# Softmax denominators summed on four quarters of TensorE's columns, inverted on 128 columns, and broadcast through DRAM

## The chip, the cores and the metric

The kernel runs on one core of a Trainium2 chip. The metric is the device time of one execution in microseconds (us). A core has five engines that work side by side, each through its own instructions in order: TensorE (PE in the profile; its weight loads are the row PEld), VectorE (DVE), ScalarE (ACT), GpSimd (POOL) and SyncE (SP), which here only issues DMAs. An instruction that has to wait holds up everything behind it on its own engine.

## The reference

Two attention layers follow each other on `x` of shape (8, 512, 64, 64), in float32. The first is a softmax attention with pooled keys and values:

```python
f = conv1x1(x, Wf, bf).reshape(b, c // K, h * w)       # 64 x 4096 for each image
g = maxpool2x2(conv1x1(x, Wg, bg))                     # 64 x 1024
v = maxpool2x2(conv1x1(x, Wh, bh))                     # 256 x 1024
s = jnp.einsum('bcn,bcm->bnm', f, g)
beta = jax.nn.softmax(s, axis=-1)
o = jnp.einsum('bcm,bnm->bcn', v, beta)
x1 = gamma * conv1x1(o, Wv, bv) + x
```

The second is a linear attention on the result x1: its features are `10 * relu(q) + exp(10 * min(q, 0))`, and `x1 + gamma * (KV applied to the features, over their norm)` is the output. The change concerns the softmax of the first layer alone: for each position n, the exponentials of 1024 scores are summed, the sum is inverted, and all 1024 are multiplied by the inverse.

## The kernel before, in words

**Chunks and steps.** Each image's 4096 positions are cut into 8 chunks of 512 (`CH`), so there are 64 chunks (`TOTAL`) in 8 images. A loop over `step(s)` runs from s = -9 to 64. A step does several stages for different chunks: `project` and `attend` of chunk s; `weigh_two`, `sum_of_e`, `total`, `invert` and `normalize_block` of the next chunk n = s + 1; the first convolutions (`a_fg`, `a_h`) of chunk s + 9; and, with j = s % 8 the step's place in its image, in steps with odd j from the second image on, `finish`, which adds the second layer's result for two chunks of the image before to the output in DRAM. The last image's eight steps have no first convolutions, since no chunk is left for them, and its own second layer is finished after the loop. Here "odd step" means a step with odd j that has a `finish`.

**What sets the order.** The order is written by hand. Every piece of work is entered by `at(t, fn, ...)`, with t a time within the step, and the step emits all of it in order of t, under a manual schedule. So the order on each engine and in each queue is the order of the t's, and the numbers t matter only as an order. The dependencies (semaphores) are put in by the framework.

**The softmax of chunk n.** `weigh` makes scores on PE, two blocks at a time, and ACT takes their exponentials into `E`, an SBUF tile of 128 partitions x 8 blocks x 512 positions: the 1024 keys lie over partitions and blocks, the positions along the columns. `sum_of_e` (L432 to L437, DVE) adds the eight blocks into `r`, 128 x 512. `total` (L441) sums `r` over the partitions by a matmul with a 128 x 128 matrix of ones, so that each of 128 partitions of a PSUM bank `tot` receives the same 512 sums. `invert` (L446) takes the reciprocal of that bank into another PSUM bank, `rtot`. `look` (L450, L451, ACT) reads both banks once more for a later check that all sums and inverses are of a sane size, and `normalize_block` (L460, DVE) multiplies the four quarters of `E` by `rtot`.

**Around it in the same step.** On PE, L441 stands among the products of `attend` (L484); after those come the convolution `fg` (L259), the products N of `project` (L547) mixed with H (L303), and then `features` (`pk`, L593). On DVE, the reciprocal is followed by nine small operations of `attend` (L502 to L517), the first quarter of L460, the pooling of `fg` (L236, L267), two quarters of L460, a sum into `xb` (L563), the last quarter, three more L563 and two L568. `features` reads `xb` after L568. On ACT, `look` is followed by the evictions of `project` (L557) with the bias added, each of which POOL adds to `xb` (L560); three later products of `project` accumulate on the bank that an eviction has read. In the last image's steps `features_exp` (L603, L604) stands between `look` and the first eviction.

**The queues.** SP issues the loads of x (L212, L224), the stores (L574) and the DMA transposes of halves: of v (`turn_v`, L358), of x (L648) and of k (L630). `turn_v` is SP's next work after the point where the change puts its DMAs. The two accumulating DMAs of `finish` (L801, 1 MB each, `out_dram<-y`) are issued by POOL. In the profile's DMA lines q1 is the queue of SP's DMAs and q0 that of POOL's.

**Buffers.** PSUM is a pool of 8 banks (`bank`), and `scratch` is a pool of 7 SBUF tiles of 128 x 512.

Of the kernel before, what the change touches and what calls it, by code (L numbers as in the profile page):

```python
# [36 lines left out]
F32 = mybir.dt.float32  # L37
U16 = mybir.dt.uint16
AF = mybir.ActivationFunctionType
ALU = mybir.AluOpType  # L40
AX = mybir.AxisListType

PARAM = 10.0
EPS = 1e-10
P = 128
CH = 512
SAFE = 1e27

# [2 lines left out]
def tile_two_attention_blocks(  # L51
# [21 lines left out]
    nc = tc.nc  # L73
# [3 lines left out]
    CV = WhT.shape[1]  # L77
    KT = C // P
    VT = CV // P
    NCHUNK = N // CH  # L80
    M = N // 4
    MT = M // P
    NT = CH // P
    TOTAL = B * NCHUNK
    HN = CH // 2
    xr = x.rearrange("b (k p) h w -> b p k (h w)", p=P)
    outr = out.rearrange("b (k p) h w -> b p k (h w)", p=P)
    wv1r = wvT.rearrange("(k p) o -> p k o", p=P)

    const = ctx.enter_context(tc.tile_pool(name="const", bufs=1))  # L90
# [23 lines left out]
    for e in range(2):  # L114
        nc.scalar.dma_start(out=b_kq[e * D : (e + 1) * D, e : e + 1], in_=bk.rearrange("(p o) -> p o", o=1))
        nc.scalar.dma_start(
            out=b_kq[(1 - e) * D : (2 - e) * D, e : e + 1], in_=bq.rearrange("(p o) -> p o", o=1)
# [6 lines left out]
    ident = const.tile([P, P], F32, name="ident")  # L124
# [4 lines left out]
    ones = const.tile([P, P], F32, name="ones")  # L129
    nc.gpsimd.memset(ones, 1.0)  # L130

    kk = const.tile([P, CH], F32, name="kk")

# [29 lines left out]
    chk = const.tile([P, 2, TOTAL], F32, name="chk")  # L163
# [4 lines left out]
    def run(ctx, general):  # L168
# [6 lines left out]
        work1 = ctx.enter_context(tc.tile_pool(name="work1", bufs=1))  # L175
        work = ctx.enter_context(tc.tile_pool(name="work", bufs=2))
        temp = ctx.enter_context(tc.tile_pool(name="temp", bufs=7))
        turned = ctx.enter_context(tc.tile_pool(name="turned", bufs=1))
        small = ctx.enter_context(tc.tile_pool(name="small", bufs=4))
        psum = ctx.enter_context(tc.tile_pool(name="psum", bufs=8, space=bass.MemoryType.PSUM))  # L180

        def bank(name):
            return psum.tile([P, CH], F32, tag="m", name=name)

        def scratch(name):
            return temp.tile([P, CH], F32, tag="t", name=name)

# [38 lines left out]
        st = {}  # L226
        fgs, fs, vps = {}, {}, {}

        th, hs, es, sums, totals, rtots, te, os_, to, ns = ({} for _ in range(10))
        pxs, x_last, stored, late = [], {}, {}, {}  # L230
        kTs, xTs, pks, qq, halves, turned_halves = ({} for _ in range(6))

# [204 lines left out]
                nc.vector.tensor_tensor(r[:, 0, :], r[:, 0, :], r[:, 1, :], ALU.add)  # L437

        def total(s):
            pt = totals[s] = bank(f"tot_{s}")  # L440
            nc.tensor.matmul(pt, ones, sums[s][:, 0, :], start=True, stop=True)  # L441

        def invert(s):

            rtots[s] = bank(f"rtot_{s}")
            nc.vector.reciprocal(rtots[s], totals[s])  # L446

        def look(s):
            pt = totals[s]
            nc.scalar.activation(pt, pt, AF.Copy, accum_out=chk[:, 0, s : s + 1])  # L450
            nc.scalar.activation(pt, rtots[s], AF.Copy, accum_out=chk[:, 1, s : s + 1])  # L451

        def block(s, i, j):

# [438 lines left out]
        def step(s):  # L893
# [8 lines left out]
            def at(t, fn, *args):  # L902
                work.append((t, len(work), fn, args))
# [79 lines left out]
            if after:  # L983
                n = s + 1
                if here:
                    at(5.7, weigh_two, n, 0)
                    at(7.5, weigh_two, n, 2)
                    for m, t in ((2, 9.3), (4, 10.6), (6, 11.8), (8, 13.1)):
                        at(t, sum_of_e, n, m)

                if not here:
                    t, t_invert = 21.2, 21.25
                elif s == 0:
                    t, t_invert = 21.2, 22.6
                else:
                    t, t_invert = 16.1 if j % 2 == 1 and c_here else 17.85, 18.0
                at(t, total, n)
                at(t_invert, invert, n)
                if not general:
                    at(max(21.5, t_invert + 0.1), look, n)  # L1000
                at(24.3, normalize_block, n, 0, 1)
                at(26.0, normalize_block, n, 0, 0)
                at(27.3, normalize_block, n, 1, 1)
                at(29.2, normalize_block, n, 1, 0)
                at(33.6, sums_of_e, n, 1)
                at(36.0, sums_of_e, n, 2)
# [65 lines left out]
        for s in range(-LEAD, TOTAL + 1):  # L1072
            step(s)
# [5 lines left out]
    with ExitStack() as stack, tc.manual_schedule(engines=ENGINES):  # L1079
        run(stack, general=False)  # L1080

    least = const.tile([1, 1], F32, name="least")
    good = const.tile([1, 2 * TOTAL], F32, name="good")
    nc.vector.tensor_scalar(good, chk[0:1].rearrange("p c s -> p (c s)"), SAFE, None, ALU.is_lt)
    nc.vector.tensor_reduce(least, good, AX.X, ALU.min)
    bad = const.tile([1, 1], mybir.dt.int32, name="bad")
    nc.vector.tensor_scalar(bad, least, 0.5, None, ALU.is_lt)
    again = nc.values_load(bad, min_val=0, max_val=1, skip_runtime_bounds_check_because="0 or 1")
    with tc.If(again > 0):
        with ExitStack() as stack, tc.manual_schedule(engines=ENGINES):  # L1090
            run(stack, general=True)
# [37 lines left out]
```

## Time and profile before

| what | value |
|---|---|
| median of 3 runs | 2661.5 us (2658.37 to 2662.64) |
| the profiled execution | 2656.62 us, span 2654.5 us, granted TensorE clock 0.994 |
| busy: PE, PEld, DVE, ACT, POOL | 2606.4, 1798.1, 2136.8, 1593.2, 763.5 us |
| L441, PE, 128 x 512, two passes for each of 64 | 128 passes, 592 ns each as recorded |
| L446, DVE, reciprocal 128 x 512 | 64, 3365 ns each |
| L450 and L451, ACT, 128 x 512 | 64 each, 589 and 582 ns |
| L460, DVE, 128 x 1024 | 256, 1214 ns each |
| L801, accumulating DMAs of 1 MB | 56, median 11.4 us from issue to landing |

The span runs from the first to the last instruction. A float32 matmul appears as two passes, each with a weight load. A pass of 512 columns is recorded with 592 ns, but in a stream the next starts 0.43 us later; the chain of waits counts the latter.

### The profile page before, as it was taken

The page shows a single profiled execution, that of the slowest core. Times are in us where ns is not written, and L with a number is a line of the kernel's source. Part 1 is how long each engine was busy: PE and PEld are TensorE (multiplying, and loading weights), DVE is VectorE, ACT ScalarE, POOL GpSimd, SP SyncE. Part 2 cuts the span into 40 slices and gives each one's busy share as a digit, 9 for nine tenths or more (in the row PEclk, how much of TensorE's full clock was granted, in tenths as well). Part 3 has the DMA queues.
Part 4 walks back from the last instruction along what each step waited for, and adds up shares of the span by engine and source line. Part 5 has one row for each costly group of instructions (what it writes and reads, how often), then busy time and mean ns, then how long its engine had stood idle before and what let it go on. Part 6 is the DMA issues. An engine that isn't in the chain of part 4 may idle for free.

```text
span 2654.5 us, 30415 instructions
## 1 busy us (share of the span) xinstructions
PE 2606.4 (98%) x10650; PEld 1798.1 (68%) x10650; DVE 2136.8 (80%) x2990; ACT 1593.2 (60%) x2670; POOL 763.5 (29%) x610
## 2 busy tenths in 40 slices
PE   8899999999999999999999999999999999999996
PEld 6577666667667667667667676666676676666663
DVE  5788879878888878887888888888788788798873
ACT  3365566566566566575675665666665656756661
POOL 4422323322322323223333223323223232221112
PEclk9999999999999999999999999999999999999998
DMA  5143455465555565655664654756555656455657
GB/s 172 49 134 89 115 135 149 104 164 134 133 157 118 142 167 118 164 133 116 152 162 121 155 125 123 180 116 151 141 118 158 155 119 159 117 138 138 154 144 256
DMA packets 465363, 369.91 MB, mean 139 GB/s; under 512 B 339888, under 2 KB 340400, under 8 KB 465200
## 3 DMA queue, kind: packets, MB, share of 16 engines
q1 hardware_dynamic: 444816, 307.16, 42.6%
q0 software_dynamic: 15232, 58.72, 12.0%
q10 hardware_dynamic: 5152, 1.97, 0.3%
q8 instruction: 87, 1.43, 0.2%
q14 instruction: 76, 0.62, 0.1%
HBM read 151.92 MB, written 134.22 MB: 108 GB/s over the span
## 4 chain that ended last, share of the span: by engine, by line
PE 87%; DVE 6%; DMA 1%; issue 1%; ACT 1%; POOL 0%; SPq 0%; DVEq 0%; POOLq 0%; ACTq 0%
PE M L484 27%; PE N L547 14%; PE H L303 11%; PE s L394 8%; PE pk L593 7%; PE fg L259 7%; PE pg L687 4%; PE pa L795 3%; PE tot L441 2%; PE pkv L752 1%; PE pd L770 1%; DMA xb<-in_x_dram 1%; DVE T L469 1%; DVE T L466 1%; DVE r L434 0%
## 5 line engine op out<-in xcount | busy, mean ns | idle before, releaser
L560 POOL TENSOR_TENSOR xb<-xb,n 128x512 f32<-128x512 f32 x192 | 246.7, 1285 | 553.3 <-ACT n L557 504.2
L484 PEld LDWEIGHTS M<-T,S 128*128 128x128 f32 x1536 | 286.5, 190 | 114.3 <-issue 29.2
L557 ACT ACTIVATE n<-N,gb_v 128x256 f32<-128x256 f32 x384 | 161.2, 471 | 334.1 <-PE N L547 333.2
L484 PE MATMUL M<-T,S 128*128 128x256 f32 x1536 | 358.7, 383 | 0.0
L655 ACT COPY xT<-u 128x1024 uint16<-128x1024 uint16 x252 | 328.2, 1353 | 1.4
L460 DVE TENSOR_TENSOR E<-E,rtot 128x1024 f32<-128x1024 f32 x256 | 305.2, 1214 | 3.8 <-issue 1.6
L642 ACT COPY w<-xb 128x1024 uint16<-128x1024 uint16 x252 | 244.8, 1042 | 81.8 <-DVE xb L563 81.8
L398 ACT ACTIVATE E<-s 128x512 f32<-128x512 f32 x512 | 256.1, 615 | 48.3 <-PE s L394 40.6
L446 DVE RECIPROCAL rtot<-tot 128x512 f32<-128x512 f32 x64 | 215.3, 3365 | 49.4 <-PE tot L441 49.4
L547 PE MATMUL N<-to,w_v 128*128 128x256 f32 x1024 | 243.6, 381 | 3.2 <-ACT n L557 3.0
L563 DVE TENSOR_TENSOR xb<-xb,N 128x512 f32<-128x512 f32 x256 | 175.0, 684 | 84.2 <-POOL xb L560 81.9
L394 PE MATMUL s<-f,g 64*128 64x512 f32 x1024 | 238.1, 602 | 1.9 <-DVE o L493 1.9
L593 PE MATMUL pk<-xb,w_kqk 128*128 128x512 f32 x512 | 231.8, 595 | 8.0 <-DVE xb L568 8.0
L634 POOL COPY kT<-uk 128x512 uint16<-128x512 uint16 x56 | 53.1, 949 | 620.6 <-DMA uk<-wk 620.6
L484 PE MATMUL M<-E,vT 128*128 128x256 f32 x1024 | 231.5, 379 | 0.0
L450 ACT ACTIVATE tot<-tot 128x512 f32<-128x512 f32 x64 | 37.7, 589 | 320.0 <-DVE rtot L446 319.9
L547 PEld LDWEIGHTS N<-to,w_v 128*128 128x128 f32 x1024 | 194.3, 191 | 30.8 <-ACT n L557 4.4
L484 PEld LDWEIGHTS M<-E,vT 128*128 128x128 f32 x1024 | 194.6, 190 | 29.4 <-issue 1.9
L259 PE MATMUL fg<-xa,w_fg 128*128 128x512 f32 x472 | 213.9, 596 | 0.0
L547 PE MATMUL N<-o,w_v 128*128 128x256 f32 x768 | 187.7, 380 | 1.9 <-ACT n L557 1.9
L547 PEld LDWEIGHTS N<-o,w_v 128*128 128x128 f32 x768 | 145.1, 190 | 54.8 <-issue 24.2
L394 PEld LDWEIGHTS s<-f,g 64*128 64x128 f32 x1024 | 94.7, 186 | 116.5 <-issue 90.6
(149 smaller groups left out, 4647.8 us busy)
## 6 DMA issues: line engine op xcount, KB each, us to landing
xb<-in_x_dram SPq DMA_DIRECT2D x64, 1024.0 KB, 5.7
out_dram<-xb SPq DMA_DIRECT2D x64, 1024.0 KB, 5.3
xa<-in_x_dram SPq DMA_DIRECT2D x59, 1024.0 KB, 7.4
out_dram<-y POOLq DMA_DIRECT2D x56, 1024.0 KB, 11.4
w_v<-in_L_conv_wv_dram SPq DMA_DIRECT2D x8, 1024.0 KB, 8.1
x_early<-in_x_dram SPq DMA_DIRECT2D x4, 1024.0 KB, 5.7
u<-w SPq DMA_TRANSPOSE x252, 3.3
x<-out_dram SPq DMA_DIRECT2D x12, 256.0 KB, 10.7
```

The costliest lines, as they stand in the source:

```text
L259: nc.tensor.matmul(fg, w_fg[:, k, :], x_a[a][:, k, :], start=(k == 0), stop=(k == KT - 1))
L303: nc.tensor.matmul(m[i], w_h7[i][:, k, :], th[a][i][:, k, :], start=(k == 0), stop=(k == hk - 1))
L394: nc.tensor.matmul(sc[e], g[half(e), i, :], fs[s][half(e), :], start=True, stop=True)
L398: nc.scalar.activation(es[s][:, 2 * i + e, :], sc[e], AF.Exp)
L446: nc.vector.reciprocal(rtots[s], totals[s])
L460: nc.vector.tensor_tensor(b, b, r, ALU.mult)
L484: nc.tensor.matmul(m[i], v7[i][:, k, :], te[s][i][:, k, :], start=(k == 0), stop=(k == hm - 1))
L547: nc.tensor.matmul(a[:, k, :], w_v7[i][:, bass.ts(k, P)], b, start=not more and k == 0, stop=True, skip_group_check=more or k > 0,)
L560: nc.gpsimd.tensor_tensor(of_x(*ij), of_x(*ij), u, ALU.add)
L593: nc.tensor.matmul(pk, w_kqk[:, i, e * D : (e + 2) * D], x_b[s][:, i, :], start=(i == 0), stop=(i == KT - 1),)
L642: nc.scalar.copy(w, x_b[s][:, k, :].bitcast(U16).rearrange("p (n h) -> p h n", h=2))
L655: nc.scalar.copy(v[:, k], u)
```

## The change

`total` becomes four matmuls instead of one. Each has a 128 x 32 slice of the matrix of ones and 128 of the 512 positions, and writes 32 partitions of the first 128 columns of `tot`; so partitions 0 to 31 hold the sums of the first 128 positions, 32 to 63 those of the next 128, and so on. `invert` takes the reciprocals of these 128 x 128 values into an SBUF tile `rq`. Two DMAs on SP follow (`spread_inverses`): four rows of `rq` go to a small DRAM tile, and from there the 512 inverses are read back into all 128 partitions of a `scratch` tile. ACT then copies that to the PSUM bank `rtot` (`keep_inverses`), which `normalize_block` reads as before. `look` reads 128 instead of 512 columns. Because the partitions now hold different sums, the closing test reads all partitions of `chk` and takes their minimum with one transpose on PE and one more reduction.

```diff
+QP = 32
...
+        rows = ctx.enter_context(tc.tile_pool(name="rows", bufs=2, space=bass.MemoryType.DRAM))
...
         def total(s):
-            pt = totals[s] = bank(f"tot_{s}")
-            nc.tensor.matmul(pt, ones, sums[s][:, 0, :], start=True, stop=True)
+
+            pt = totals[s] = bank(f"tot_{s}")[:, 0:P]
+            for i in range(NT):
+                nc.tensor.matmul(
+                    pt[bass.ts(i, QP), :], ones[:, 0:QP], sums[s][:, 0, bass.ts(i, P)],
+                    start=True, stop=True,
+                )
 
         def invert(s):
-
-            rtots[s] = bank(f"rtot_{s}")
-            nc.vector.reciprocal(rtots[s], totals[s])
+            rq[s] = work1.tile([P, P], F32, tag="rq", name=f"rq_{s}")
+            nc.vector.reciprocal(rq[s], totals[s])
+
+        def spread_inverses(s):
+
+            d = rows.tile([NT, P], F32, tag="rd", name=f"rd_{s}")
+            nc.sync.dma_start(out=d, in_=rq[s][0:P:QP, :])
+            u = rtots[s] = scratch(f"rb_{s}")
+            nc.sync.dma_start(out=u, in_=d.rearrange("(o i) n -> o (i n)", o=1).to_broadcast([P, CH]))
+
+        def keep_inverses(s):
+            u, rtots[s] = rtots[s], bank(f"rtot_{s}")
+            nc.scalar.copy(rtots[s], u)
 
         def look(s):
             pt = totals[s]
             nc.scalar.activation(pt, pt, AF.Copy, accum_out=chk[:, 0, s : s + 1])
-            nc.scalar.activation(pt, rtots[s], AF.Copy, accum_out=chk[:, 1, s : s + 1])
+            nc.scalar.activation(pt, rq[s], AF.Copy, accum_out=chk[:, 1, s : s + 1])
...
                 at(t, total, n)
                 at(t_invert, invert, n)
+                at(t_invert + 0.01, spread_inverses, n)
+                at(max(23.0, t_invert + 0.02), keep_inverses, n)
                 if not general:
                     at(max(21.5, t_invert + 0.1), look, n)
                 at(24.3, normalize_block, n, 0, 1)
...
-    least = const.tile([1, 1], F32, name="least")
-    good = const.tile([1, 2 * TOTAL], F32, name="good")
-    nc.vector.tensor_scalar(good, chk[0:1].rearrange("p c s -> p (c s)"), SAFE, None, ALU.is_lt)
+    least = const.tile([P, 1], F32, name="least")
+    good = const.tile([P, 2 * TOTAL], F32, name="good")
+    nc.vector.tensor_scalar(good, chk.rearrange("p c s -> p (c s)"), SAFE, None, ALU.is_lt)
     nc.vector.tensor_reduce(least, good, AX.X, ALU.min)
+    with tc.tile_pool(name="row", bufs=1, space=bass.MemoryType.PSUM) as last:
+        row = last.tile([1, P], F32, name="row")
+        nc.tensor.transpose(row, least, ident)
+        nc.vector.tensor_reduce(least[0:1], row, AX.X, ALU.min)
     bad = const.tile([1, 1], mybir.dt.int32, name="bad")
-    nc.vector.tensor_scalar(bad, least, 0.5, None, ALU.is_lt)
+    nc.vector.tensor_scalar(bad, least[0:1], 0.5, None, ALU.is_lt)
```

More of the change, by code (lines that the diff above doesn't have):

```diff
@@ L227, in run @@
         fgs, fs, vps = {}, {}, {}
-        th, hs, es, sums, totals, rtots, te, os_, to, ns = ({} for _ in range(10))
+        th, hs, es, sums, totals, rq, rtots, te, os_, to = ({} for _ in range(10))
         pxs, x_last, stored, late = [], {}, {}, {}
```

## The prediction, made before the changed kernel was run

> **What bounds the kernel now.** I read the page's busy row and its chain of waits first, then the chain of one odd step in order of time, then DVE's timeline of that step, because DVE is where the long reciprocal goes.
>
> ```profile
> PE 2606.4 (98%) x10650; PEld 1798.1 (68%) x10650; DVE 2136.8 (80%) x2990; ACT 1593.2 (60%) x2670; POOL 763.5 (29%) x610
> ...
> PE 87%; DVE 6%; DMA 1%; issue 1%; ACT 1%; POOL 0%; SPq 0%; DVEq 0%; POOLq 0%; ACTq 0%
> ```
>
> ```profile
> 1274.86 1.93 PE M L484 x8
> 1276.79 0.86 PE tot L441 x2
> 1277.65 5.18 PE M L484 x24
> ...
> 1286.26 4.32 PE N L547 x20
> ...
> 1296.62 3.43 PE pk L593 x8
> ```
>
> ```profile
> 1277.75 3.37 DVE L446 RECIPROCAL rtot<-tot 128x512 f32<-128x512 f32 x1 [0.50 <-PE tot L441]
> ...
> 1284.78 1.21 DVE L460 TENSOR_TENSOR E<-E,rtot 128x1024 f32<-128x1024 f32 x1
> 1286.30 0.69 DVE L236 TENSOR_REDUCE gp<-fg 64x128 f32<-64x512 f32 x1 [0.31 <-PE fg L259]
> ...
> 1291.98 1.41 DVE L563 TENSOR_TENSOR xb<-xb,N 128x512 f32<-128x512 f32 x2 [0.57 <-POOL xb L560]
> 1294.57 0.69 DVE L563 TENSOR_TENSOR xb<-xb,N 128x512 f32<-128x512 f32 x1 [1.18 <-POOL xb L560]
> 1295.17 0.87 DVE L568 SCALAR_TENSOR_TENSOR xb<-N,gb_v,xb 128x256 f32<-128x256 f32 x2
> ```
>
> PE follows PE without a gap; in the steady part of the run (300 to 2330 us) its only pauses are some 0.45 us once per image. So the 0.86 us of L441 are on the path, the 3.37 us of the reciprocal are not. But DVE runs close behind: from the first L460 to the end of L568 it idles only 0.31 + 0.57 + 1.18 us, and L568 ends (1296.04) about 0.58 us ahead of pk. Where a matmul did wait for DVE (L437 ending at 2390.85), it began 0.14 us later; I allow 0.3 for that hand-over, so 0.28 of these are free. An odd step can take 0.31 + 0.57 + 1.18 + 0.28 = 2.34 us of delay at its first L460. In an even step only one idle of 0.85 us stands there, so it can take 0.85 + 0.28 = 1.13.
>
> **What the Trainium skill says.** "TensorE: Matmul & The Clock Gate", Part 3 (packing small matmuls), measures 2.38x for three column tiles and 3.07x for four row tiles. The trace shows two column tiles at work: pg's eight passes (L687, 64 columns of the array each) take 1.87 us, where eight passes in series take 3.43 (pk). "DMA: Bandwidth & Descriptors", Anatomy of one DMA, gives about 2 us fixed for a DMA from GpSimd, most of it the receipt of the write; this trace agrees for SP: the transpose uk lands 2.6 us after its issue, 1.19 of them the issue. The same page, Rules for kernel authors: a DMA that reads what another wrote must wait for its semaphore; so the change's two latencies add up. And under Queues, rings and completion order: the DMA engines take turns between queues, so POOL's accumulating DMAs delay SP's. The trace shows by how much. First the transpose uv in an even step, then in an odd one, then the queues over 1276 to 1281 and 1281 to 1286 us:
>
> ```profile
> uv<-wv SPq DMA_TRANSPOSE x1, 3.2
> ```
>
> ```profile
> uv<-wv SPq DMA_TRANSPOSE x1, 11.7
> ```
>
> ```profile
> q0 software_dynamic: 254, 1.00, 103.2%
> ```
>
> ```profile
> q0 software_dynamic: 243, 0.97, 97.5%
> q1 hardware_dynamic: 209, 0.05, 8.4%
> ```
>
> uv, issued at 1276.18, has no packet on q1 until 1281.0; uk, alone, has its first 1.2 us after its issue. So a newcomer waits 3.6 us behind q0, then gets about one packet for each of q0 (some 0.33 us), until q0 runs dry at about 1286.5.
>
> **The change, part by part.**
>
> 1. *Four quarter sums* (on the path). Before 0.86. After: each quarter has two passes of 128 columns, 2 x 0.43/4 = 0.21 us, the four side by side. Filling and emptying costs what pg shows, 1.87 - 4 x 0.43 = 0.15. So 0.36, a gain of 0.50 in each of 62 steps where PE is on the path: **-31 us**. Bounds: pairwise overlap only, 0.43 + 0.15, gain 0.28 (-17); no overlap, 0.86 + 0.15, a loss of 0.15 (+9).
>
> 2. *Reciprocal of 128 columns*: 3.37/4, about 0.85. The 2.5 us saved on DVE free the nine operations behind it, which then wait for PE's M products; nothing on the path becomes earlier.
>
> 3. *Two DMAs on SP, in series*. No row shows such small ones. Issue to first packet: 0.9 (the store of xb, issued at 1262.93, behind uk). DMA 1 (2 KB): 0.9, plus write and receipt, 2.0 in all, between 1.6 and 3. DMA 2 (256 KB, 128 rows of 2 KB, eight per DMA engine at 0.08): 2.4, between 2 and 3.5. Behind them on SP waits only turn_v (uv), whose reader join_v comes some 16 us later: nothing. ACT's copy costs 0.58 (L451's 582 ns); look loses 2 x 384 columns, about 0.6: nothing net on ACT. *keep_inverses* is a new wait: behind it on ACT stand the evictions L557, and PE's third following product accumulates on the bank they read; behind L460 stands DVE's chain to pk.
>
>  *Even steps and those without finish*: reciprocal end to L460: 2.0 + 2.4 + 0.58 + 0.35 for four hand-overs = 5.35. The reciprocal starts 0.5 earlier with PE. Step of 1237.52: 1237.02 + 0.85 + 5.35 = 1243.2; before, moved by PE's 0.5, 1243.66. **0**. The cover is 0.45 + 1.13 = 1.6 us; beyond it, each us costs 36 us in all.
>
>  *Odd steps* (23 with all stages). Reciprocal 1277.3 to 1278.15; DMA 1 could show packets at 1279.1, waits behind q0 as uv did, to about 1282.7, lands at 1283.8. DMA 2 could start at 1284.7, but finds the rest of q0; its last engine is free at 1286.2, eight rows 0.65, receipt 0.4: 1287.2. Copy and hand-overs 0.76: L460 at 1287.96. Before, with PE's 0.5: 1284.28. Late by 3.68, less 2.34: a stall of 1.34 us, 23 times: **+31**. Bounds: if q0 and q1 alternate from the start, DMA 2 lands at 1285.6 and nothing is left (0); if it is last of all like uv, at 1287.9, 2.0 (+47).
>
> 4. *Last image and the step before.* There is no fg or H to fill in. n = 56: DVE is already the path (L460 starts on L517's heels), so the lateness counts whole: +3.4. n = 58, 60, 62: q0 begins 1.9 us later against the total, and features_exp and the eviction stand behind the copy: some 2.2 each. **+10** (4 to 15).
>
> 5. *The first two steps*: DVE and ACT are the path there. L460 follows the reciprocal's start by 4.9 us now, by 0.85 + 5.35 = 6.2 after: **+3**.
>
> 6. *The end*: transpose and reduction run while seven stores land: 0, at most +1.
>
> Sum: -31 + 31 + 10 + 3 = +13, from the profiled 2656.6 to 2669.6. The median of the runs lies 4.9 above that execution, so I state **2674**. What replaces PE's own work on the path is, in odd steps, DMA 2 -> ACT's copy -> L460 -> L568 -> pk.
>
> **The rivals.**
>
> - *The inverses slip past the accumulating DMAs* (ends faster). The stall of the odd steps is nearly none, and the quarters' gain stays: 2661.5 - 31 + 8 (part 4's lower end, part 5, a trace of stall) = **2638**. For it: q0 and q1 do alternate once both run. Against: uv's 3.6 us without a packet. It turns faster than before when the broadcast lands before about 1286.7 in that step, only half a us ahead of my 1287.2.
> - *The even steps stall too.* If the two DMAs and the copy take 8 us instead of 5.35, 1 us over the cover, 36 x 1 on top: **2710**. For it: a store to DRAM and a load back is a path this trace never takes, and other small DMAs at the start of the kernel land in 4 to 7 us, beside big ones. Against: q1 is empty from 1238 to 1245.
> - *The quarters don't overlap.* Part 1 becomes +9 (pairwise -17): **2688 to 2714**. Against: pg.
>
> **How the numbers follow.** Forecast 0.46 (2655 to 2692), slipping past 0.24, even steps stall 0.18, no overlap 0.12. What a measurement can tell from no change is 0.2%, 5.3 us: 2656.2 to 2666.8. Of the forecast I put 0.14 there and nothing below; of slipping past all but 0.01 is faster. The others are slower. So faster 0.23, same 0.15, slower 0.62. Range 2634 to 2712: under it lies the best third of the first rival (0.08), over it the worse half of the second and the worst of the third (0.12).
>
> **What would show it.** Part 1: tot's eight passes take about 0.36 us in PE's chain and DVE's idle ahead of the reciprocal stays short. Part 3: L460 starts in even steps within 6.5 us of the reciprocal's start and PE has no gap; in odd steps some 10.5 us after it, and pk or the N products wait for DVE or ACT by 1 to 1.5 us. I am wrong if rb lands before q0's last packets in odd steps, if even steps show gaps on PE, or if tot takes 0.6 us or more.

## The result, and the profile after

| kernel | median | runs |
|---|---|---|
| before | 2660.5 us | 4 (2658.37 to 2662.64) |
| after | 2721.7 us | 4 (2715.59 to 2723.95) |

The ratio is 1.0226, with a 95% interval from 1.0207 to 1.0245: the change makes the kernel slower by 61 us. The forecast said slower, at 2674, and its range ended at 2712. The profiled execution of the kernel after took 2722.3 us, its span 2720.2, at a granted clock of 0.990.

The page of the kernel after, its busy row and the shares of its chain of waits:

```profile
PE 2611.7 (96%) x11035; PEld 1780.7 (65%) x11035; DVE 2011.2 (74%) x2991; ACT 1590.3 (58%) x2734; POOL 758.0 (28%) x610
...
PE 70%; DMA 11%; DVE 8%; ACT 3%; issue 3%; POOL 1%; SPq 0%; DVEq 0%; POOLq 0%; ACTq 0%
```

DVE has lost 126 us of work, and the kernel is slower. The chain, which was PE for 87%, now runs over DMAs for 11% (before 1%) and over DVE and ACT for another 11% (before 7%). So the wait for the inverses is no longer hidden. Which wait it is can be read in the view of waits of the kernel after (engine, what it waited for, us in total, times, longest):

```profile
ACT rtot L463 <- DMA rb<-rd: 378.4, 64, 10.0
DVE E L477 <- ACT rtot L463: 178.6, 63, 6.5
...
PE N L564 <- ACT n L574: 60.0, 55, 4.6
ACT f L279 <- DVE gp L238: 40.5, 31, 1.8
```

ACT stands at its copy for up to 10 us. The third row is the price: PE, which before waited for nothing in the steady part, waits for ACT's evictions 55 times, 46 of them in the 23 odd steps of the steady part, two in each.

The chain of waits shows one odd step of the kernel after in order of time (start, us, what):

```profile
1293.39 1.93 PE M L501 x8
1295.31 0.40 PE tot L445 x8
...
1295.74 0.97 DVE rq L452
...
1296.72 5.30 DMA rd<-rq
...
1302.08 4.80 DMA rb<-rd
...
1306.90 0.60 ACT rtot L463
...
1307.52 1.22 DVE E L477
...
1308.78 0.71 DVE gp L238
...
1309.51 0.68 ACT f L279
...
1310.89 0.85 ACT n L574 x2
...
1311.78 1.13 PE N L564 x4
```

The eight passes of the sums take 0.40 us up to their last result. From the reciprocal's start to L477, the old L460, it is 11.78 us; the prediction had 10.66, and before it was 7.03. Then the chain leaves DVE by another door than the forecast one: the pooling `gp`, ACT's two `f` copies that need it, the eviction that stands behind them, and the product N that needs its bank. `pk` waits for nothing here.

The even step just ahead of it, on DVE's timeline (start, us, operation, idle before it):

```profile
1255.88 0.96 DVE L452 RECIPROCAL rq<-tot 128x128 f32<-128x128 f32 x1 [0.85 <-PE tot L445]
...
1262.35 1.22 DVE L477 TENSOR_TENSOR E<-E,rtot 128x1024 f32<-128x1024 f32 x1 [1.00 <-ACT rtot L463]
```

There it is 6.47 us, and PE has no gap. What differs is what the accumulating DMAs do to the queues; the experiments below test it. First the DMA queues of the kernel after over 1303 to 1304 us, then over 1304 to 1305 and over 1305 to 1306 (packets, MB, share of the 16 engines); DMA 2 was issued at 1302.08:

```profile
q0 software_dynamic: 54, 0.22, 110.7%
```

```profile
q1 hardware_dynamic: 86, 0.14, 59.4%
q0 software_dynamic: 27, 0.05, 24.9%
```

```profile
q1 hardware_dynamic: 394, 0.18, 139.1%
```

In the first of these microseconds SP's queue q1 moves nothing at all. Its packets come as POOL's q0 runs dry: q0's last packet of 4 KB ends at 1304.73, and the broadcast lands at 1306.88, 2.15 us later.

To see where the 65.7 us between the two profiled spans lie, I cut each execution at the start of the reciprocals of chunks 1, 9, 55 and 63. The stretch from 9 to 55 holds 46 full steps, 23 of them odd; that from 55 to 63 is the last image. The other rows are experiments told below.

| us | to n=1 | 1 to 9 | 9 to 55 | 55 to 63 | rest | span |
|---|---|---|---|---|---|---|
| before | 127.6 | 301.1 | 1857.5 | 262.8 | 105.6 | 2654.5 |
| after | 132.1 | 299.7 | 1895.7 | 284.5 | 108.2 | 2720.2 |
| no trip (e3) | 127.3 | 296.1 | 1843.0 | 259.7 | 108.2 | 2634.3 |
| accumulating a step later (e1) | 132.7 | 299.8 | 1853.4 | 284.5 | 115.8 | 2686.2 |
| accumulating after the trip (e5) | 130.7 | 299.8 | 1843.5 | 288.4 | 116.3 | 2678.7 |
| `f` later (e7) | 129.5 | 299.8 | 1879.4 | 285.8 | 105.6 | 2700.1 |
| hybrid (e9) | 127.7 | 298.2 | 1843.1 | 264.4 | 106.9 | 2640.3 |
| trip in odd n only (e10) | 129.8 | 301.5 | 1849.4 | 263.9 | 107.3 | 2651.8 |
| before, accumulating moved (e11) | 126.8 | 300.4 | 1857.5 | 262.8 | 108.0 | 2655.5 |

Except in e1 and e5, the last part varies between 105.6 and 108.2 in kernels with and without the change, so I read nothing from its 2.6 us.

### The profile page after: what moved, and what is told of

Same layout as the page of the kernel before. It is cut to its first block, busy times and chain, and to the rows that moved or that the text cites. A ratio compares the mean times of both kernels' runs of the same rounds, so it can differ in the third digit from the quotient of the medians.

```text
span 2720.2 us, 31486 instructions
## 1 busy us (share of the span) xinstructions
PE 2611.7 (96%) x11035; PEld 1780.7 (65%) x11035; DVE 2011.2 (74%) x2991; ACT 1590.3 (58%) x2734; POOL 758.0 (28%) x610
## 4 chain that ended last, share of the span: by engine, by line
PE 70%; DMA 11%; DVE 8%; ACT 3%; issue 3%; POOL 1%; SPq 0%; DVEq 0%; POOLq 0%; ACTq 0%
PE M L501 21%; PE H L305 10%; PE N L564 10%; PE s L396 8%; PE pk L610 7%; DMA rd<-rq 6%; DMA rb<-rd 5%; PE pg L704 4%; PE fg L261 4%; PE pa L812 3%; DVE E L477 2%; DVE rq L452 1%; ACT f L279 1%; PE pd L787 1%; PE pkv L769 1%
## 5 line engine op out<-in xcount | busy, mean ns | idle before, releaser
L477 DVE TENSOR_TENSOR E<-E,rtot 128x1024 f32<-128x1024 f32 x256 | 306.1, 1217 | 185.2 <-ACT rtot L463 178.6
L577 POOL TENSOR_TENSOR xb<-xb,n 128x512 f32<-128x512 f32 x192 | 244.9, 1276 | 628.0 <-ACT n L574 609.8
L501 PE MATMUL M<-T,S 128*128 128x256 f32 x1536 | 365.8, 388 | 0.0
L564 PE MATMUL N<-to,w_v 128*128 128x256 f32 x1024 | 257.9, 391 | 58.3 <-ACT n L574 58.1
L463 ACT COPY rtot<-rb 128x512 f32<-128x512 f32 x64 | 37.7, 589 | 378.4 <-DMA rb<-rd 378.4
L305 PE MATMUL H<-xa,w_h 128*128 128x256 f32 x708 | 171.7, 379 | 0.0
```

Of the source, the lines that this page charges most:

```text
L305: nc.tensor.matmul(m[i], w_h7[i][:, k, :], th[a][i][:, k, :], start=(k == 0), stop=(k == hk - 1))
L477: nc.vector.tensor_tensor(b, b, r, ALU.mult)
L501: nc.tensor.matmul(m[i], v7[i][:, k, :], te[s][i][:, k, :], start=(k == 0), stop=(k == hm - 1))
L564: nc.tensor.matmul(a[:, k, :], w_v7[i][:, bass.ts(k, P)], b, start=not more and k == 0, stop=True, skip_group_check=more or k > 0,)
L577: nc.gpsimd.tensor_tensor(of_x(*ij), of_x(*ij), u, ALU.add)
```

## The experiments

My theory after the result: the round trip costs only because its DMAs wait behind the accumulating ones, and ACT's evictions wait behind the copy. The rivals: the trip's traffic or SP's queue costs; DVE's shorter reciprocal has hidden worth; the quarters themselves bring nothing. Four of the kernels (e1 to e4) ran beside 9 runs of the kernel before with a median of 2657.4 us, four (e5 to e8) beside 9 with 2659.2, and the last three beside 21 with 2659.1.

**The quarters alone (e2).** The kernel before, with four matmuls of 32 columns each over all 512 positions:

```diff
-            nc.tensor.matmul(pt, ones, sums[s][:, 0, :], start=True, stop=True)
+            for i in range(NT):
+                nc.tensor.matmul(
+                    pt[bass.ts(i, 32), :], ones[:, 0:32], sums[s][:, 0, :], start=True, stop=True)
```

> The kernel before, with the one matmul of total replaced by four on the four quarters of the columns, each over all 512 positions, so that every partition still gets all sums and nothing else changes. It measures only what it costs PE to enter and leave the quarters. Theory (0.15 us of filling and 0.20 us that the stream after it loses, as the trace of the changed kernel shows): 0.35 x 62 = +22 us, 2682. If entering and leaving cost only the 0.15 of my prediction: +9, 2669. If the quarters do not overlap: four times 0.86 instead of once, +160, 2820.

Measured: 2680.1 us, ratio 1.008 (1.0067 to 1.0094), 22.7 us more, as expected. The array's work is the same 0.86 us of streaming, so some 0.35 us per step are the price of going into the quarters and out of them. The prediction counted 0.15. The other 0.20 could have been read from the chain of the kernel before:

```profile
1231.11 1.87 PE pg L687 x8
1232.97 3.65 PE M L484 x16
1236.62 0.86 PE tot L441 x2
1237.48 3.45 PE M L484 x16
```

The 16 passes behind `pg`, which works on half the columns at a time, take 3.65 us, the same 16 behind the whole matmul 3.45. In the kernel after they take 3.65 behind `tot` as well. The chain counts all of the 0.20 behind the group; by the starts of the passes about half of it (0.09 us) lies ahead of the four quarters and half (0.10) behind them.

**No trip (e3).** The DMAs are left out; ACT copies `rq`, repeated four times, to `rtot`:

```diff
-                at(t_invert + 0.01, spread_inverses, n)
...
-            nc.scalar.copy(rtots[s], u)
+            nc.scalar.activation(rtots[s].rearrange("p (i n) -> p i n", n=P),
+                rq[s].unsqueeze(1).to_broadcast([P, NT, P]), AF.Copy, scale=1e-30)
```

> The changed kernel without the two DMAs: ACT fills the bank of inverses straight from the 128 columns of reciprocals, repeated four times and scaled by 1e-30 (the output is left wrong by that: the inverses don't reach the right partitions). PE, DVE and ACT have the same instructions as in the changed kernel. Theory (all of the loss is the wait for the two DMAs, and the quarters gain 0.30 us net per step): 2660 - 18 + 3 = about 2645 us. Rival (the quarters cost PE more than they save): 2700 or more. If the quarters gain 0.50 net as predicted: 2632.

Measured: 2637.3 us, ratio 0.9921 (0.9905 to 0.9937). So the trip costs 84 us of the kernel after, and all else that the change does brings some 20. In the table's middle stretch that is (1857.5 - 1843.0)/46 = 0.32 us per step: 0.50 for the shorter stream less the 0.20 for leaving the quarters.

**The DMAs without a reader (e8).** As e3, with both DMAs issued as in the kernel after, into a tile that nobody reads:

```diff
+                at(t_invert + 0.01, spread_inverses, n)
...
+            u = scratch(f"rb_{s}")
```

> The kernel without the trip (e3_no_trip), but with the two DMAs issued at their place on SP and landing in a scratch tile that nobody reads (the output is left wrong as in e3_no_trip). Traffic, SP's queue and turn_v behind it are as in the changed kernel; only the wait of ACT and DVE is gone. Theory (the wait alone costs): as e3_no_trip, 2637 us, within 5. Rival (the trip's traffic, or v's transpose behind it on SP, costs time by itself): 2660 or more.

Measured: 2635.1 us, ratio 0.991 (0.9895 to 0.9925). With the same traffic and the same queue on SP the 84 us are gone. So the loss is the wait for the data and what follows from it, not the traffic.

**DVE's load put back (e6).** As e3, with a second reciprocal of 384 columns:

```diff
+            more = scratch(f"more_{s}")
+            nc.vector.reciprocal(more[:, 0:384], sums[s][:, 0, 0:384])
```

> The kernel without the trip (e3_no_trip), with a second reciprocal of 128 x 384 values, read by nobody, behind the first, so that DVE has its 3.4 us back (the output is left wrong as in e3_no_trip). Theory (DVE's relief is worth nothing, only the quarters save time): as e3_no_trip, 2637 us, within 4. Rival (the relief of DVE is part of the 20 us that e3_no_trip gains on the kernel before): 2647 or more.

Measured: 2633.8 us, ratio 0.9904 (0.9889 to 0.992). The 126 us that DVE was relieved of are worth nothing here, as the prediction said.

**The accumulating DMAs a step later (e1).** They are collected and issued at 20.5 of the following step, except for an image's last pair:

```diff
-            at(t + 3.4, out)
+            if jp < NCHUNK // 2 - 1:
+                due.append(out)
+            else:
+                at(t + 3.4, out)
```

> The changed kernel, with the two accumulating DMAs of finish issued by POOL in the following step, after the first convolution's sums, instead of in the step itself (not for the last pair of an image). 18 of the 23 full odd steps and three of the last image's then have no accumulating DMA beside the broadcast. Theory (the inverses wait behind the accumulating DMAs): each of these 18 steps loses its 2.3 us, the three in the last image some 5 us each: 2722 - 41 - 15 = about 2666 us. Rival (any trip through DRAM stalls the step, whatever else is on the queues): no change, 2722. Rival (the quarter matmuls themselves cost PE the time): no change, 2722.

Measured: 2686.6 us, ratio 1.0101 (1.0082 to 1.012). The mechanism shows: in the middle stretch the moved steps have no gap, and 10.4 us are left over e3, for the five pairs that were not moved, 2.1 each. But the last image, which was to give back 15 us, keeps its whole loss, and the rest grew by 7.6. There the steps are short, and in those of chunks 59, 61 and 63 PE had gaps of 5.5 to 6.8 us. At chunk 59 the moved DMAs hold up SP's four transposes of x for 14.1 us. SP's store and load of x come late behind these, and the trip's first DMA, behind the store and the load, takes 6.88 us, while the view of the DMA queues over 2431 to 2434 us has SP's queue alone:

```profile
q1 hardware_dynamic: 436, 0.87, 100.3%
```

So the trip also waits behind large transfers of its own queue.

**After the trip in the same step (e5).**

```diff
-            at(t + 3.4, out)
+            s = (b + 1) * NCHUNK + 2 * jp + 1
+            at((20.5 if s + LEAD < TOTAL else 31.5 if s < TOTAL - 1 else t + 3.4)
+               + 0.05 * ks[0], out)
```

> The changed kernel, with the accumulating DMAs of finish issued in the same step, but behind the broadcast: POOL issues them after the first convolution's sums (t = 20.5; in the last image and the step before it, where those sums are missing, at 31.5). All odd steps then have a broadcast with nothing beside it. Theory (the wait behind the accumulating DMAs is the whole loss): the 23 full odd steps give back 2.3 us each, the last image some 18: 2722 - 53 - 18 = about 2651 us, under the kernel before by what the quarters save. Rival (the trip costs more than the quarters save even alone, or the accumulating DMAs now hold up the transposes of x): 2670 or more.

Measured: 2680.5 us, ratio 1.0082 (1.0068 to 1.0095). The middle stretch, 1843.5, is that of e3 to half a us: with the accumulating DMAs out of its way the trip is free in every full step. The miss is again the last image, where I had chosen 31.5. Its chain of waits for chunk 56:

```profile
2326.09 1.93 POOL out_dram L818 x2
2328.01 12.65 DMA u<-w
...
2348.09 2.55 PE s L396 x4
```

Now the transposes of x stand behind the accumulating DMAs, for 12.65 us, and PE's scores wait. At chunks 59, 61 and 63 the trip again comes late behind them, as in e1, and PE has gaps of 5.2 to 7.0 us. Neither of the two places that were tried keeps the two DMAs of 1 MB out of the way in a short step.

**`f` later (e7).** ACT's `f` copies are entered at 31.5, behind the evictions:

```diff
-                a_fg(a, at, 21.3, 28.35 if c_here and here and j == 0 else 26.0)
+                a_fg(a, at, 21.3, 31.5 if here else 26.0)
```

> The changed kernel, with ACT's two copies of f placed behind the third eviction (t = 31.5 instead of 26.0 or 28.35). In the changed kernel they wait in odd steps for the pooling of fg on DVE, which stands behind the first normalize_block, and the second eviction waits behind them. Theory (0.8 to 1.1 us of the 2.3 of an odd step come this way): -0.8 x 23 = about 2703 us. Rival (the DVE chain to pk would be next at once): 2722 less no more than 5. Over 2722 if the fg bank, held longer, makes a product wait.

Measured: 2703.5 us, ratio 1.0174 (1.0155 to 1.0194). The middle stretch falls by 16.3 us, 0.71 for each odd step: so much went through `gp` and `f`. Its chain in an odd step shows what is left:

```profile
1297.57 0.59 ACT rtot L463
1298.16 0.78 ACT n L574 x2
...
1298.98 1.99 PE N L564 x8
```

The first pair of evictions stands directly behind the copy, and PE behind them. The second pair is no longer late.

**No copy (e4).** `normalize_block` reads the tile in SBUF; ACT copies nothing, and so ACT doesn't wait at all:

```diff
-                at(max(23.0, t_invert + 0.02), keep_inverses, n)
```

> The changed kernel without ACT's copy: normalize_block reads the broadcast inverses from the SBUF scratch tile. ACT then waits for no DMA, DVE still does. Theory (the larger part of an odd step's stall comes over ACT: the first eviction waits behind the copy, and the product that accumulates on its bank waits for it, 1.2 us; the rest comes over DVE, the pooling and the f copy): -1.2 x 23 = -28 and some -10 in the last image, about 2685 us. Rival (the stall comes over DVE and pk, as I predicted): only the copy's 0.6 us, -14 and little in the last image, about 2705. If multiplying from SBUF made the 128x1024 product slower, more than 2722.

Measured: 2734.1 us, ratio 1.0287 (1.0263 to 1.031): slower than the kernel after, against my expectation. Two groups of the page of e4 show what became slower (busy, mean ns of one, idle before):

```profile
L477 DVE TENSOR_TENSOR E<-E,rb 128x1024 f32<-128x1024 f32 x256 | 384.8, 1525 | 138.7 <-DMA rb<-rd 137.9
L577 POOL TENSOR_TENSOR xb<-xb,n 128x512 f32<-128x512 f32 x192 | 288.4, 1502 | 584.3 <-ACT n L574 563.8
```

In the kernel after these are 1217 and 1276 ns. The pooling stands behind the first L477, so ACT's `f` copies wait for `gp` 84.2 us in all, instead of 40.5, and the evictions behind them. Sorted by whether an L577 of POOL runs at the same time, L477 of e4 has a median of 1.58 us (179 of them, up to 2.30) with one and of 1.23 (77) without; in the kernel after it is 1.22 in both cases. The Trainium skill gives a reason, in "SBUF — State Buffer", SBUF: two separate sides: DVE and GpSimd share a pair of ports as an exclusive lock, and a DVE operation with two SBUF inputs contends for it with a GpSimd operation that reads SBUF. This agrees: the loser then waits for what is left of the other's operation, and the longest L477 here lost 1.08 us, less than one L577. So the copy to PSUM, which looks like a needless step, keeps DVE and POOL out of each other's way. The experiment does not tell what ACT's wait alone is worth, since it brought this second cost with it.

**The trip where it is free (e9).** As e5 for the full steps, with the trip and the quarters for chunks 2 to 55 only; the first two and the last image take the old path, their accumulating DMAs at the old place:

```diff
+        def trip(s):
+            return 2 <= s < TOTAL - NCHUNK
...
+            if not trip(s):
+                pt = totals[s] = bank(f"tot_{s}")
+                nc.tensor.matmul(pt, ones, sums[s][:, 0, :], start=True, stop=True)
+                return
...
+            at((20.5 if s + LEAD < TOTAL else t + 3.4) + 0.05 * ks[0], out)
```

> The kernel after, with the accumulating DMAs of out issued at 20.5 of the same step where a later image still has work, and with the quarters and the round trip only for n = 2 to 55; n = 0, 1 and 56 to 63 take the whole matmul and the 512 reciprocals of the kernel before. Nothing is left out. Theory (the trip costs only where it meets an accumulating DMA or a step with too little work beside it; a full step then keeps the 0.30 us that two steps of e5 gained against before, 78.9 for 79.49 us): 54 steps x 0.30 = 16 us below before, 2643. Rival (the trip takes something in every step, which e5's steps hid in some other gain): 2655 to 2662, no better than before. A second rival (the gain belongs to the later accumulating DMAs, not to the quarters): the control that moves them alone in the kernel before shows the same gain.

Measured: 2642.3 us (5 runs, 2641.56 to 2647.07), ratio 0.9941 (0.9927 to 0.9954). It beats both kernels and is within 1 us of the expectation. Its last image is 1.6 us longer than before's; 3.41 us at half the clock, which before does not have there, would account for it. Its waits:

```profile
ACT rtot L473 <- DMA rb<-rd: 210.1, 54, 4.6
...
PE N L574 <- ACT n L584: 2.9, 4, 0.9
```

ACT still stands 3.9 us at each copy, and nobody stands behind it: PE's 60.0 us have become 2.9.

**The accumulating DMAs moved in the kernel before (e11).** The control for e9: the last line of its diff alone.

> The kernel before, with its accumulating DMAs of out issued at 20.5 of the same step, as in e9; nothing else changed, nothing left out. Theory (nothing in the kernel before waits for these DMAs): 2659 within 4. Rival (their place costs something there already, which e5 and e9 gain too): 2645 to 2652, and then the gain of the hybrid is this and not the quarters.

Measured: 2657.5 us, ratio 0.9996 (0.9988 to 1.0005). Their place is worth nothing without the trip, so the gain of e9 is that of the quarters.

**The trip in the steps without accumulating DMAs (e10).** `trip(s)` is `2 <= s and s % 2 == 1`, the DMAs stay where they were.

> The kernel after, with the quarters and the round trip only for the odd n from 3 on (31 steps, those in which no accumulating DMA is issued); the even n and n = 1 as in the kernel before. The accumulating DMAs stay where they were. Nothing is left out. Theory (the trip alone is hidden behind the other work of such a step): 31 x 0.30 = 9 us below before, 2650, and no N product waits longer than in before. Rival (the trip costs in those steps too, a little in each): 2659 or above. Second rival (the switch between 512 and 128 columns of inverses from step to step costs DVE or PSUM buffers): some 2665.

Measured: 2650.6 us, ratio 0.9971 (0.9961 to 0.9981), as expected. The trip alone is hidden in an even step, with no other edit, and the switching to and fro costs nothing that shows.

## Why the prediction was wrong, point by point

The sign was right, and so was the mechanism in the main: the two DMAs wait behind the accumulating ones, and only in odd steps and where there is little other work. What failed are four sizes and, in the odd steps, the path by which the wait reaches PE. With e3 the sum can be taken apart: after less e3 is the wait, e3 less before is the rest.

| term | predicted | measured |
|---|---|---|
| quarters, and everything but the wait | -31 | -20.2 (2634.3 - 2654.5) |
| odd steps | +31 | +52.7 (1895.7 - 1843.0) |
| last image | +10 | +24.8 (284.5 - 259.7) |
| first steps | +3 | +8.4 (4.8 to n=1, 3.6 from there to n=9) |
| end | 0 to +1 | 0.0 (108.2 - 108.2; e3 has the changed end too) |
| sum | +13 | +65.7 |

*Part 1, quarters.* They do overlap, and the 0.36 us was exact where PE's own work follows. The step that failed is the gain of 0.50: it ended the count with the last pass, where the stream behind loses another 0.20. Measured 0.32, within the stated bounds, and 11 us of the miss.

*Part 2, reciprocal.* 0.96 us, not 0.85, and nothing on the path (e6).

*Part 3, even steps.* L477 follows the reciprocal's start by 6.47, forecast 6.2; nothing is lost (e5's and e9's middle stretch, e10). That the sum fits so well is partly luck: DMA 1 takes 1.6 instead of 2.0, DMA 2 3.2 instead of 2.4.

*Part 3, odd steps.* This is the step that failed most, 22 us. The sequence was right: DMA 1 waits for q0, then DMA 2 does. DMA 1's 5.65 was near (5.30), and q0 ended about when it was to. The term that failed is what DMA 2 needs behind q0: 0.65 for its rows and 0.4 for the receipt, 1.05 in all. From q0's end to the landing it took 2.15. The rows are what was mis-sized, and the even step shows it with nothing of q0 beside them. The view of the DMA queues there, over 1258 to 1260.2 us and over 1260.2 to 1261.4 us:

```profile
DMA packets 70, 0.13 MB, mean 59 GB/s; under 512 B 4, under 2 KB 8, under 8 KB 70
```

```profile
DMA packets 514, 0.24 MB, mean 201 GB/s; under 512 B 448, under 2 KB 448, under 8 KB 514
```

Of DMA 2's 128 rows of 2 KB, 62 start in the first of these stretches and 66 in the second, the first at 1259.48 and the last at 1261.26: 1.8 us, not 0.65. In the second stretch they share q1 with small packets, which come with the transposes of v; the rows of the first stretch, without those, came at a rate that would make some 1.5 us for all 128 (an estimate). In the even step the cover hid this.

L477 is therefore 4.75 late against before (11.78 - 7.03) and not 3.68, and the stall is 52.7/23 = 2.29 instead of 1.34. The route was wrong too: I took DVE's chain to `pk`, with 2.34 us to spare, and named ACT's evictions as standing behind the copy without counting them. They bind first. That 4.75 less 2.34 gives nearly the measured stall is a coincidence. In the odd step of e7 shown above L477 is 4.49 late, the two N gaps have become one of about 1.0 us, and `pk` still does not wait, so DVE's chain can take some 3 us; `pk` begins at 1307.20, before the second of the two sums that end that chain is through (1307.26), so the count to the end of L568 was too strict. Still, that chain is close behind: in the odd step of the kernel after DVE works from L477 to the end of L585, the old L568, without a pause, and ends 0.58 us ahead of `pk`, as before. Without ACT's route, most of the stall would probably have come by the forecast one; no run shows it.

*Part 4, last image.* The prediction counted lateness at 2.2 to 3.4 a step; PE's gaps behind the copy are 4.65 at chunk 56 and 2.76, 3.87 and 3.11 at 58, 60 and 62, 14.4 us in all. A second cost is on top. The view by windows of the kernel after, for the time of that first gap and behind it (us; busy us of PE, PEld, DVE, ACT, POOL; granted clock):

```profile
2376.00:2379.80 3.80, 0.63 (x3) 0.58 (x4) 1.42 (x2) 1.36 (x3) 0.59 (x1) 1.00 0.35 62
2379.80:2383.20 3.40, 3.40 (x10) 2.69 (x9) 3.40 (x4) 0.84 (x2) 1.95 (x2) 0.50 0.00 0
```

Behind each of these four gaps PE runs at half its clock for 3.4 us, at chunk 56 once more after its next waits, so up to 1.7 us are lost again each time. With these five windows 22.9 of the 24.8 us are accounted for, as an estimate. The Trainium skill describes it in "TensorE: Matmul & The Clock Gate", Part 1 (the clock gate): after an idle window of some 3.4 us the clock is halved, until a window of that length has been busy. A single gap of 2.76 us was enough here. In e9 two gaps of 0.93 and 1.34 us close together, at chunk 56, were followed by such a window too, in e3 the same two were not. Neither the prediction nor its range had this slower clock.

*Parts 5 and 6.* Part 5 was for two steps, and they hold all of this row: up to n=1 4.8, and then the 3.6, which lie in the next step alone. From the reciprocal of chunk 1 to that of chunk 2 it is 35.9 us against 31.9 in e3, and PE waits 2.42 us for an eviction there; behind it the steps of the first image differ by less than 1 us. Against before, to which the forecast of 3 belongs, these two steps cost 4.7 (4.5 and 0.2), since PE waited 3.0 us for the same eviction there already. The term is uncertain by a few us: to n=1 it is 126.8 to 129.8 in rows without a trip there. The end costs nothing that shows: the last part of the table lies in the same range with the changed end and with the old one.

*The rivals.* The inverses do not slip past the accumulating DMAs, the even steps do not stall, and the quarters overlap; none of the three is what happened. The range failed in its terms. All upper bounds together, -17, +47, +15, +3 and +1, give 2710.5 with the median's 4.9, and the measured odd steps (52.7), last image (24.8) and first steps (8.4) lie above theirs by 21 us in all. The bound on the last image had no room for a slower clock behind each delay; the one on the odd steps let DMA 2 end no later than the transposes of v had.

## What to carry to other kernels

A wait through DRAM has no fixed price: the same two DMAs took 4.8 us in one step and 10.1 in the next, for what stood in the other queue, and the first of them 6.88 us behind large transfers of its own queue. So look first for what else the DMA engines carry at that time, and move that, where there is room; in the steps without room, keep the old path. When an instruction waits in the middle of an engine's order, follow every instruction behind it to its reader, not only the chain of the data. And read the price of an operation in the chain up to the end of what follows it.

## What the runs showed of the hardware

- Four matmuls on 32 columns each run fully side by side (eight passes of 128 columns in 0.36 us), but the stream of full-width passes around them loses 0.20 us, and with the 0.15 of filling a switch costs 0.35 (e2: 22.7 us over 62 steps).
- A DVE product of 128 x 1024 takes 1.22 us with one operand in PSUM, with or without a sum of POOL's beside it; with both in SBUF (e4) it takes 1.23 alone and 1.58 (up to 2.30) beside one.
- Waits of PE of 2.8 us and more in the last image were followed by 3.4 us at half the clock (kernel after), and once two of 0.93 and 1.34 us close together (e9).
- A 2 KB store to DRAM took 1.6 us to the issue of the load that waits for it, the 256 KB broadcast back another 3.2; behind accumulating DMAs of another queue 5.3 and 4.8 (kernel after).
- The broadcast's 128 rows of 2 KB took 1.8 us from the first start to the last with nothing of another queue beside them, and in the second half the transposes of their own (kernel after, even step).
